# One hybrid convolution, scan and spectral block: the third image's block products split by source, the last block in two halves, and a wider carry on GpSimd

## The chip, the cores and the metric

The kernel runs on one core of one Trainium2 chip. The metric is device time in microseconds (us). The kernel before takes 21922.89 us, the median of three runs from 21910.68 to 21937.1; the profiled execution took 21922.63 us and its trace spans 21920.9 us.

## The reference, cut to what matters

Four images of 128 channels and 64 x 64 pixels pass through two layers. Layer 0 (group norm, two depthwise convolutions, a sort of patches, a scan with 16 states per channel) is not touched. In layer 1 each image is a row of 4096 tokens of 128 channels, and two things are computed, one after the other:

```
t = t + attn(ln(t))
    xs, z = split(ln(t) @ W_in);  delta = xs @ W_delta;  Bv = xs @ W_B;  Cv = xs @ W_C
    state[d, n] = exp(delta[d] * A[d, n]) * state[d, n] + delta[d] * Bv[n] * xs[d]   # token by token
    y[d] = sum over n of state[d, n] * Cv[n];   out = (y * silu(z)) @ W_out
t = t + stu(ln(t))
    U[k] = causal convolution of the tokens with filter phi[:, k], k = 0..15, and the same with
           alternating signs
    out  = sum over k of U_plus[k] @ M_plus[k] + U_minus[k] @ M_minus[k]   (+ a 3-tap term)
```

There are 256 x 256 states per token. The causal convolution of 4096 tokens is done as block products: output block `blk` (1024 tokens) takes a product with each source block from 0 to `blk`.

## The kernel before, in words

**The loop over scans.** After layer 0, `layer1` takes each image in eight chunks of 512 tokens, so 32 "parts" in all, and each part in 256 steps, one for each of 256 channels d. A step is one scan instruction on VectorE over 2 x 512 elements (L1110, `s<-da,v`): 128 partitions by two halves hold the 256 states, and 512 tokens run along the row. 8192 steps make the main loop. For every step other engines make its inputs ahead of it:

- SyncE fetches a broadcast row of `delta` for two steps (`dlb<-delta`, L1084, four buffers), issued eight steps ahead.
- GpSimd multiplies it with `u` into `v` for two steps (`spread`, L1098, one instruction over 128 x 2044 elements, three buffers), four steps ahead. ScalarE then puts the first column of each row into `v` (L1102).
- ScalarE makes the factors `da` by two exponentials (`lift`, L1107), one step ahead, in two PSUM buffers.
- The state crosses from one part to the next in `last`. `carry` (L1092, L1093) folds it into `af` and `vf` on GpSimd, 32 channels at a time, six steps ahead, so eight times in every part but the first of an image.

After each group of eight steps TensorE contracts the scanned states with `C` (L1127, `yp<-s,c`), ScalarE copies the result out (L1133, `ye`, one buffer), and a DMA stores it (L1134).

**The work beside it.** A generator, `beside`, does the projections of the next part and the output of the last one in small pieces between the steps. A piece of kind "free" is given at any step, one of kind "mm" only at the seventh step of a group of eight. Layer norms (`normalise`) go through GpSimd for the power -0.5 (L772, L773) and then on ScalarE (L777), two "free" pieces later.

**The spectral work.** When the output of a second chunk is done, `block` puts tasks on a queue. A task is (image, block, sources, partly, full): `partly` says that a sum from an earlier task is added at its end, `full` that the block is complete after it; a task that isn't full writes its sum to DRAM. A task has 64 items (2 rows r x 16 filters x 2 sides). An item is, for each source, four conv matmuls of up to 512 columns (L1058) against a strip of the filter from DRAM (L975, three buffers); then a copy of the PSUM tile on ScalarE (L1069), and one matmul with the mixing matrix `pq` (L969, five buffers) into `fin` (L1002). Images 0 to 2 take all sources of a block in one task, so nothing of block 3 can start before the image's last chunk is through. The last image (`b == NB - 1`) takes most sources as tasks of their own, so that work on blocks 2 and 3 starts with block 0. The products of the source that is the block itself are triangular: 512, 384, 256 and 128 columns.

**What sets the order.** The order is written out by hand: the engines run their instructions in the order in which this Python loop emits them. At each step the loop takes matmuls from the generator `products` until a credit is used up. The credit is `pace` x 512 columns a step, with pace 1.4 for parts 0 to 19 and 1.7 from part 20 on. After the last step, `go_on` emits what is left of the queue; this stretch, after the last scan, is called the tail below. All loads go through the one SyncE queue in program order.

Of the kernel before, what the change touches and what calls it, by code (L numbers as in the profile page):

```python
# [8 lines left out]
F32 = mybir.dt.float32  # L9
# [6 lines left out]
NB = 4  # L16
# [591 lines left out]
TS = 512  # L608
NCH = L // TS
NT = TS // 128  # L610
GD = 8
# [78 lines left out]
def layer1(ctx: ExitStack, tc, ident, half, w_in, w_delta, w_b, w_c, w_out, a_t, phi, pqd, mud, x2, x3, out):  # L690
# [66 lines left out]
    def normalise(t):  # L757

        st = sm.tile([128, NT, 6], F32, tag="st", name="st")
        mv = sm.tile([128, NT, 2], F32, tag="mv", name="mv")  # L760
        for i in range(NT):
            nc.vector.bn_stats(st[:, i, :], t[:, i, :])
        for i in range(NT):
            nc.vector.bn_aggr(mv[:, i, :], st[:, i, :])
        yield "free"
        ve = sm.tile([128, NT], F32, tag="ve", name="ve")
        nc.scalar.activation(ve, mv[:, :, 1], AF.Identity, bias=eps)
        ms = sm.tile([128, NT], F32, tag="ms", name="ms")
        nc.scalar.activation(ms, mv[:, :, 0], AF.Copy, scale=-1.0)
        yield "free"  # L770
        rs = sm.tile([128, NT], F32, tag="rs", name="rs")
        nc.gpsimd.tensor_tensor(rs, ve, half[:, :NT], ALU.pow)  # L772
        nc.gpsimd.tensor_tensor(ms, ms, rs, ALU.mult)  # L773
        yield "free"
        yield "free"
        for i in range(NT):
            nc.scalar.activation(  # L777
                t[:, i, :], t[:, i, :], AF.Identity, bias=ms[:, i : i + 1], scale=rs[:, i : i + 1]
            )
# [91 lines left out]
    def output(b, ch, yt, gate):  # L871


        cols = bass.ts(ch, TS)
        xr = small()
        nc.sync.dma_start(xr, x2[b][:, cols])
        yk = wide()
        nc.sync.dma_start(yk, gate)
        for k in range(2):
            yield "mm"  # L880
            ps = middle()
            for i in range(NT):
                nc.tensor.transpose(ps[:, bass.ts(i, 128)], yt[:, i, bass.ts(k, 128)], ident)
            yield "post"
            nc.vector.tensor_tensor(yk[:, k, :], ps, yk[:, k, :], ALU.mult)
        yield "mm"
        ps = middle()
        for k in range(2):
            nc.tensor.matmul(ps, wo[:, k, :], yk[:, k, :], start=k == 0, stop=k == 1)
        yield "post"  # L890
        nc.vector.tensor_tensor(xr, xr, ps, ALU.add)
        yield "mm"
        pair = xr.rearrange("p (a q) -> p q a", q=2)
        tp = middle()
        for r in range(2):
            for i in range(2):
                nc.tensor.transpose(tp[:, bass.ts(2 * r + i, 128)], pair[:, r, bass.ts(i, 128)], ident)
        yield "post"
        tk = small()
        nc.scalar.copy(tk, tp)  # L900
        yield "free"
        yield from normalise(tk.rearrange("p (i c) -> p i c", i=NT))
        yield "mm"
        if ch % 2 == 0:
            tokens[b, ch // 2] = sp.tile([128, 2, 4, 128], F32, tag="tok", name="tok", bufs=5)
        tok = tokens[b, ch // 2]
        ps = middle()
        nc.tensor.matmul(ps, flip, tk, start=True, stop=True)
        yield "post"
        nc.scalar.copy(tok[:, :, bass.ts(ch % 2, 2), :], ps.rearrange("p (r i c) -> p r i c", r=2, i=2))  # L910
        yield "mm"
        up = middle()
        for i in range(NT):
            nc.tensor.transpose(up[:, bass.ts(i, 128)], tk[:, bass.ts(i, 128)], ident)
        mu = sm.tile([128, 3, 128], F32, tag="mu", name="mu", bufs=1)
        nc.sync.dma_start(mu, mud[:, (0, 1, 2, 2, 3, 3, 3, 3)[ch]])
        yield "post"
        ut = sm.tile([128, 2 + TS], F32, tag="ut", name="ut", bufs=1)
        nc.scalar.copy(ut[:, 2:].rearrange("p (a q) -> p q a", q=2), up.rearrange("p (q a) -> p q a", q=2))
        if ch:  # L920
            nc.scalar.copy(ut[:, 0:2], halo)
        else:
            nc.scalar.activation(ut[:, 0:2], ident[:, 0:2], AF.Copy, scale=0.0)
        nc.scalar.copy(halo, ut[:, TS:])
        yield "mm"
        ps = middle()
        for i in range(3):
            nc.tensor.matmul(ps, mu[:, i, :], ut[:, bass.ds(2 - i, TS)], start=i == 0, stop=i == 2)
        yield "post"
        nc.vector.tensor_tensor(xr, xr, ps, ALU.add)  # L930
        nc.sync.dma_start(x3[b][:, cols], xr)
        if ch % 2:
            block(b, ch // 2)


# [8 lines left out]
    def block(b, blk):  # L944


        if b < NB - 1:
            tasks = [(b, blk, range(blk + 1), False, True)]
        else:
            tasks = (  # L950
                [(b, 0, [0], False, True), (b, 2, [0], False, False), (b, 3, [0], False, False)],
                [(b, 1, [0, 1], False, True), (b, 2, [1], True, False), (b, 3, [1], True, False)],
                [(b, 2, [2], True, True), (b, 3, [2], True, False)],
                [(b, 3, [3], True, True)],
            )[blk]
        for task in tasks:
            queue.extend(
                (task, r, k, side, src) for r in range(2) for k in range(NK) for side in range(2) for src in task[2]
            )

    def load(i):

        (b, blk, sources, _, _), r, k, side, src = queue[i]
        if src == sources[0]:
            segs = (0, 2) if blk == 0 else (min(blk + 1, 3), 1)
            pq = sp.tile([128, 2, 128], F32, tag="pq", name="pq", bufs=5)
            nc.sync.dma_start(pq[:, 0 : segs[1]], pqd[k, side][:, bass.ds(*segs)])  # L969
            mats[i] = pq  # L970
        lo = max(0, 512 * (blk - src) - 384)
        width = 896 if src < blk else 512
        strip = sp.tile([128, 896], F32, tag="strip", name="strip")
        start = (NK + k) * row + r if side else k * row + 1
        nc.sync.dma_start(strip[:, :width], bass.AP(phi.tensor, start + lo, [[1, 128], [1, width]]))  # L975
        strips[i] = strip, lo

    def products():
# [5 lines left out]

        def finish(item):
            nonlocal fin, xo, sofar
            (b, blk, _, partly, full), r, k, side, pq, u = item
            for job in [j for j in later if j[1] is u]:
                later.remove(job)
                job[2]()  # L990
            begin, end = (k, side) == (0, 0), (k, side) == (NK - 1, 1)
            cost = TS
            if begin:
                for job in [j for j in later if j[1] == "sum"]:
                    later.remove(job)
# [2 lines left out]
                if full and r == 0:  # L998
                    xo = sp.tile([128, 2 * TS], F32, tag="xo", name="xo", bufs=1)
                    nc.sync.dma_start(xo, x3[b][:, bass.ts(blk, 2 * TS)])  # L1000
            for n, (c0, w) in enumerate([(0, 256), (256, 256)] if blk == 0 else [(0, 512)]):
                nc.tensor.matmul(  # L1002
                    fin[:, bass.ds(c0, w)], pq[:, n, :], u[:, bass.ds(c0, w)],
                    start=begin and n == 0, stop=end and not partly, skip_group_check=True,
                )
# [23 lines left out]
        while True:  # L1029
# [15 lines left out]
            while issued < len(queue) and issued < i + 3:  # L1045
                load(issued)
                issued += 1
            task, r, k, side, src = queue[i]
            b, blk, sources = task[:3]
            if src == sources[0]:  # L1050
                pq = mats.pop(i)
                ps = pc.tile([128, TS], F32, tag="conv", name="conv")
            strip, lo = strips.pop(i)
            tok = tokens[b, src]
            for j in range(4):
                skip = 128 * j if src == blk else 0
                c0 = 512 * (blk - src) - 128 * j + skip
                nc.tensor.matmul(  # L1058
                    ps[:, skip:], tok[:, 1 - r if side else r, j, :], strip[:, bass.ds(c0 - lo, TS - skip)],
                    start=src == sources[0] and j == 0, stop=src == sources[-1] and j == 3,  # L1060
                )
                if j < 3:
                    yield TS - skip
            i += 1
            if src == sources[-1]:
                u = sp.tile([128, TS], F32, tag="conved", name="conved")

                def empty(u=u, ps=ps):
                    nc.scalar.copy(u, ps)  # L1069

                later.append((now[0] + 1, u, empty))
                before, waiting = waiting, ((task, r, k, side, pq, u), now[0] + 1)
# [14 lines left out]
    def carry(ch, d, ready):  # L1087

        af, vf = ready[4:]
        cols = bass.ds(d, 32)  # L1090
        if ch:
            nc.gpsimd.tensor_tensor(af[:, :, cols], af[:, :, cols], last[:, :, cols], ALU.mult)  # L1092
            nc.gpsimd.tensor_tensor(vf[:, :, cols], vf[:, :, cols], af[:, :, cols], ALU.add)  # L1093
# [21 lines left out]
    def contract(s, c, g, keep):  # L1115
# [13 lines left out]
                    )  # L1129

        def put(j):
            ye = wk.tile([128, 2, 32, GD], F32, tag="ye", name="ye", bufs=1)
            nc.scalar.copy(ye, yp[j].rearrange("p i d t -> p i t d"))  # L1133
            nc.sync.dma_start(yd[0:128, 2 * j : 2 * j + 2], ye)  # L1134

# [53 lines left out]
                    done[m] = big.tile([128, NT, 256], F32, tag="yt", name="yt", bufs=1)  # L1189
                take(done[m])  # L1190

    for k in range(-8, steps):
        now[0] = k
        j = k + 8
        if 0 <= j < steps and j % VD == 0:
            dls[j // VD] = fetch(j % 256, ready[j // 256])
        j = k + 6
        if 0 <= j < steps and j % 32 == 0:
            carry(parts[j // 256][1], j % 256, ready[j // 256])
        j = k + 4  # L1200
        if 0 <= j < steps and j % VD == 0:
# [23 lines left out]
            kind = next(side, None)  # L1225
        if at_step == GD - 1:
            fetch_y(n, d)
        pace = 1.4 if n < 5 * NCH // 2 else 1.7
        credit = min(credit + pace * TS, pace * TS)
        while credit > 0:  # L1230
            cost = next(spectral)
# [96 lines left out]
```

## Time and profile before

| stage (from the trace) | us |
|---|---|
| layer 0 and spectral weights, up to the first spread of layer 1 | 2935.7 |
| main loop, first spread to the end of the last one | 18625 |
| tail, from the last contraction (`yp`) to the end | 351 |

| engine | busy, share of the span |
|---|---|
| VectorE (DVE) | 20589.4 us, 94% |
| GpSimd (POOL) | 20181.2 us, 92% |
| TensorE (PE) | 17505.8 us, 80% |
| ScalarE (ACT) | 15831.5 us, 72% |

The shares are averages over stages that have different limits, so they do not say which engine sets the pace. In the stages of the main loop VectorE and GpSimd are both close to full, and which of the two waits for the other has to be read from the waits. In the tail neither works. In a line of the trace an instruction's idle time before it stands in brackets with what ended it; matmuls stand as two records each[...], so that a count of 8 conv records is four matmuls.

### The profile page before, as it was taken

The numbers are of one execution on the slowest core, as the hardware profiler recorded it, in microseconds if no ns is written. First come the engines' busy times: TensorE is split into PE (matmuls) and PEld (weight loads), VectorE is DVE, ScalarE is ACT, GpSimd is POOL, SyncE is SP. The second block draws the span as 40 slices with busy tenths as digits, with TensorE's granted clock in tenths as the row PEclk, the third lists the DMA queues.
The fourth block names the chain that finished last, engine by engine and source line by source line (L and its number), as shares of the span: only waits on it lengthen the run. The fifth ranks groups of instructions, "written<-read, shape, count | busy, mean of one in ns | idle before, by whom it ended". The sixth has DMA issues, their size and how long they took to land.

```text
span 21920.9 us, 291965 instructions
## 1 busy us (share of the span) xinstructions
PE 17505.8 (80%) x98516; PEld 7675.8 (35%) x98516; DVE 20589.4 (94%) x11984; ACT 15831.5 (72%) x29148; POOL 20181.2 (92%) x5932
## 2 busy tenths in 40 slices
PE   7788844565858888877768888869498899999999
PEld 4344311232323333333323333324143344334344
DVE  6788979999999999999999999999999999999993
ACT  3677757777777777777777777777777777777773
POOL 0677769999999999999999999999999999999993
PEclk8999966676979999988979999979699999999999
DMA  0455544555756776666656777757477777777775
GB/s 31 123 139 140 140 143 150 168 181 159 215 171 217 219 222 216 219 206 193 200 185 215 221 218 219 220 180 228 154 232 217 225 232 233 231 231 230 229 227 152
DMA packets 2399968, 4238.08 MB, mean 193 GB/s; under 512 B 778200, under 2 KB 1235968, under 8 KB 2395136
## 3 DMA queue, kind: packets, MB, share of 16 engines
q1 hardware_dynamic: 2398464, 4219.40, 62.8%
q8 instruction: 776, 12.71, 0.2%
q14 instruction: 728, 5.96, 0.1%
HBM read 3600.52 MB, written 617.88 MB: 192 GB/s over the span
## 4 chain that ended last, share of the span: by engine, by line
DVE 50%; POOL 17%; PE 11%; ACT 9%; issue 7%; DMA 3%; SPq 0%; DVEq 0%; POOLq 0%; ACTq 0%
DVE s L1110 43%; POOL v L1098 17%; ACT da L1107 6%; PE conv L1058 5%; DVE states L506 3%; DMA yd<-ye 2%; PE yp L1127 2%; DVE p L510 1%; PE fin L1002 1%; ACT f L498 1%; PE y L522 1%; PE mm L415 1%; ACT t L777 0%; ACT ye L1133 0%; ACT xz L362 0%
## 5 line engine op out<-in xcount | busy, mean ns | idle before, releaser
L1098 POOL TENSOR_TENSOR v<-u,dlb 128x2044 f32<-128x2044 f32 x4096 | 18342.6, 4524 | 108.9 <-DMA dlb<-delta 89.9
L1110 DVE TENSOR_TENSOR_SCAN s<-da,v 128x1024 f32<-128x1024 f32 x8192 | 18055.4, 2269 | 384.0 <-ACT da L1107 309.2
L1107 ACT ACTIVATE da<-dlb,at 128x511 f32<-128x511 f32 x16384 | 11299.4, 690 | 2064.5 <-DVE s L1110 1599.6
L1058 PE MATMUL conv<-strip,tok 128*128 128x512 f32 (+3 forms) x20480 | 8653.9, 552 | 6.7 <-DMA strip<-in_phi 6.6
L1127 PE MATMUL yp<-s,c 128*32 128x256 f32 x65536 | 5011.0, 437 | 2958.7 <-DVE s L1110 1611.9
L1058 PEld LDWEIGHTS conv<-strip,tok 128*128 128x128 f32 x20480 | 3696.9, 193 | 4126.2 <-issue 3743.4
L1127 PEld LDWEIGHTS yp<-s,c 128*32 128x32 f32 x65536 | 1990.3, 121 | 6745.9 <-issue 1835.0
L1102 ACT COPY v<-vf 128x4 f32<-128x4 f32 x4096 | 813.3, 199 | 2262.8 <-DVE s L1110 2139.2
L484 POOL TENSOR_TENSOR v<-dx,bcb 128x1024 f32<-128x1024 f32 x512 | 1207.3, 2358 | 434.5 <-DVE states L506 427.6
L1002 PE MATMUL fin<-conved,pq 128*128 128x512 f32 (+1 forms) x3200 | 1423.6, 540 | 13.2 <-ACT conved L1069 4.4
L506 DVE TENSOR_TENSOR_SCAN states<-f,v 128x1024 f32<-128x1024 f32 x512 | 1175.9, 2297 | 173.1 <-ACT f L498 124.3
L1133 ACT COPY ye<-yp 128x512 f32<-128x512 f32 x2048 | 1185.9, 579 | 136.2 <-DMA yd<-ye 123.4
L498 ACT ACTIVATE f<-dt,an 128x255 f32<-128x255 f32 x2048 | 973.5, 476 | 419.0 <-DVE states L506 368.2
L522 PE MATMUL y<-p,ident 128*128 128x512 f32 x2048 | 1008.7, 622 | 147.3 <-DVE p L510 142.2
L1069 ACT COPY conved<-conv 128x512 f32<-128x512 f32 x1344 | 778.1, 579 | 340.4 <-PE conv L1058 339.4
L510 DVE TENSOR_TENSOR p<-states,bcb 128x1024 f32<-128x1024 f32 x512 | 627.0, 1225 | 39.3 <-DVE states L506 0.9
L1002 PEld LDWEIGHTS fin<-conved,pq 128*128 128x128 f32 x3200 | 533.3, 195 | 227.1 <-issue 165.8
L522 PEld LDWEIGHTS y<-p,ident 128*128 128x128 f32 x2048 | 370.2, 196 | 680.5 <-issue 355.7
L415 PE MATMUL mm<-ow,yg 128*32 128x128 f32 x2048 | 282.1, 297 | 106.8 <-ACT om L419 105.3
L415 PEld LDWEIGHTS mm<-ow,yg 128*32 128x32 f32 x2048 | 236.2, 139 | 213.0 <-ACT om L419 128.4
L136 POOL TENSOR_TENSOR rs<-sq,half 128x1 f32<-128x1 f32 x4 | 2.2, 559 | 329.6 <-DVE sq L134 329.6
L1018 DVE TENSOR_TENSOR xo<-xo,fin 128x512 f32<-128x512 f32 x32 | 21.3, 667 | 300.8 <-PE fin L1010 300.8
(239 smaller groups left out, 6143.4 us busy)
## 6 DMA issues: line engine op xcount, KB each, us to landing
dlb<-delta SPq DMA_DIRECT2D x4096, 512.0 KB, 4.1
strip<-in_phi SPq DMA_DIRECT2D x1536, 448.0 KB, 4.8
yd<-ye SPq DMA_DIRECT2D x2048, 256.0 KB, 4.0
bcb<-bcd SPq DMA_DIRECT2D x1024, 256.0 KB, 4.2
strip<-in_phi SPq DMA_DIRECT2D x1024, 256.0 KB, 4.3
pq<-pqd SPq DMA_DIRECT2D x1088, 64.0 KB, 3.9
yt<-yd SPq DMA_DIRECT2D x4096, 4.0 KB, 3.4
pq<-pqd SPq DMA_DIRECT2D x256, 128.0 KB, 4.1
```

What stands on the lines that cost most here:

```text
L484: nc.gpsimd.tensor_tensor(v, ready[n][2][:, :, bass.ts(i, SUB)].unsqueeze(1).broadcast_to((128, 2, 2, SUB)), bc[:, 0].unsqueeze(2).broadca ...
L498: nc.scalar.activation(factors[j % 2][:, a, k, 1:], ready[n][1][:, k, SUB * i + 1 : SUB * i + SUB], AF.Exp, scale=an[:, k, 2 * g + a : 2 * ...
L506: nc.vector.tensor_tensor_scan(states.rearrange(flat), factors[j % 2].rearrange(flat), v.rearrange(flat), 0.0, ALU.mult, ALU.add)
L510: nc.vector.tensor_tensor(p, states, bc[:, 1].unsqueeze(2).broadcast_to((128, 2, 2, SUB)), ALU.mult)
L522: nc.tensor.matmul(t.rearrange("p k t -> p (k t)"), ident, p[:, a].rearrange("p k t -> p (k t)"), start=g == 0 and a == 0, stop=False, ski ...
L1002: nc.tensor.matmul(fin[:, bass.ds(c0, w)], pq[:, n, :], u[:, bass.ds(c0, w)], start=begin and n == 0, stop=end and not partly, skip_group_ ...
L1058: nc.tensor.matmul(ps[:, skip:], tok[:, 1 - r if side else r, j, :], strip[:, bass.ds(c0 - lo, TS - skip)], start=src == sources[0] and j ...
L1098: nc.gpsimd.tensor_tensor(v[:, :, :, 1:], ready[0][:, :, 1:].unsqueeze(1).broadcast_to((128, VD, 2, TS - 1)), dl[:, :, 1:].unsqueeze(2).br ...
L1107: nc.scalar.activation(da[:, h, 1:], dl[:, d % VD, 1:], AF.Exp, scale=at[:, h, d : d + 1])
L1110: nc.vector.tensor_tensor_scan(s[:, d % GD].rearrange("p h t -> p (h t)"), da.rearrange("p h t -> p (h t)"), v[:, d % VD].rearrange("p h t ...
L1127: nc.tensor.matmul(yp[i // 2][bass.ts(q, 32), i % 2], c[:, h, t], s[:, :, h, t], start=h == 0, stop=h == 1)
L1133: nc.scalar.copy(ye, yp[j].rearrange("p i d t -> p i t d"))
```

## The change

The change has six edits:

1. The third image's blocks are queued as the last image's are, source by source, so that its products can start sooner (`b < NB - 2`).
2. In the last image, block 3's own source is taken in two halves: its first two token groups (j = 0, 1) are queued when chunk 6 is done, and only the other two (j = 2, 3), which reach columns 256 to 511 alone, are left for after chunk 7. The queue's tasks now name for each source which j they take.
3. The pace is 1.7 from part 16 on (`2 * NCH`), not from part 20.
4. `carry` takes 128 channels at once, not 32, ten steps ahead.
5. `ye` has two buffers (the pool's number), and `pq` four, not five.
6. `normalise` waits five "free" pieces, not two, between GpSimd's power and ScalarE's use of it.

```diff
@@ normalise
-        yield "free"
-        yield "free"
+        for _ in range(5):
+            yield "free"
@@ output
-        if ch % 2:
+        if (b, ch) == (NB - 1, NCH - 2):
+            add([(b, 3, [(3, range(2))], True, False)])
+        elif (b, ch) == (NB - 1, NCH - 1):
+            add([(b, 3, [(3, range(2, 4))], True, True)])
+        elif ch % 2:
             block(b, ch // 2)
@@ block
-        if b < NB - 1:
+        if b < NB - 2:
             tasks = [(b, blk, range(blk + 1), False, True)]
@@ load
-            pq = sp.tile([128, 2, 128], F32, tag="pq", name="pq", bufs=5)
+            pq = sp.tile([128, 2, 128], F32, tag="pq", name="pq", bufs=4)
@@ products
+            first = 128 * sources[0][1][0] if sources[0][0] == blk else 0
...
-            for n, (c0, w) in enumerate([(0, 256), (256, 256)] if blk == 0 else [(0, 512)]):
+            for n, (c0, w) in enumerate([(0, 256), (256, 256)] if blk == 0 else [(first, TS - first)]):
...
-            for j in range(4):
+            for j in js:
...
-                    nc.scalar.copy(u, ps)
+                    nc.scalar.copy(u[:, cols], ps[:, cols])
@@ carry
-        cols = bass.ds(d, 32)
+        cols = bass.ds(d, 128)
@@ put
-            ye = wk.tile([128, 2, 32, GD], F32, tag="ye", name="ye", bufs=1)
+            ye = wk.tile([128, 2, 32, GD], F32, tag="ye", name="ye")
@@ the loop
-    for k in range(-8, steps):
+    for k in range(-10, steps):
...
-        j = k + 6
-        if 0 <= j < steps and j % 32 == 0:
+        j = k + 10
+        if 0 <= j < steps and j % 128 == 0:
             carry(parts[j // 256][1], j % 256, ready[j // 256])
...
-        pace = 1.4 if n < 5 * NCH // 2 else 1.7
+        pace = 1.4 if n < 2 * NCH else 1.7
```

More of the change, by code (lines that the diff above doesn't have):

```diff
@@ L955, in block, with add @@
             )[blk]
+        add([(b, blk, [(src, range(4)) for src in srcs], *rest) for b, blk, srcs, *rest in tasks])
+    def add(tasks):
         for task in tasks:
             queue.extend(
-                (task, r, k, side, src) for r in range(2) for k in range(NK) for side in range(2) for src in task[2]
+                (task, r, k, side, n)
+                for r in range(2) for k in range(NK) for side in range(2) for n in range(len(task[2]))
             )
     def load(i):
-        (b, blk, sources, _, _), r, k, side, src = queue[i]
-        if src == sources[0]:
+        (b, blk, sources, _, _), r, k, side, which = queue[i]
+        src = sources[which][0]
+        if which == 0:
             segs = (0, 2) if blk == 0 else (min(blk + 1, 3), 1)
-            pq = sp.tile([128, 2, 128], F32, tag="pq", name="pq", bufs=5)
+            pq = sp.tile([128, 2, 128], F32, tag="pq", name="pq", bufs=4)
             nc.sync.dma_start(pq[:, 0 : segs[1]], pqd[k, side][:, bass.ds(*segs)])
@@ L986, in finish @@
             nonlocal fin, xo, sofar
-            (b, blk, _, partly, full), r, k, side, pq, u = item
+            (b, blk, sources, partly, full), r, k, side, pq, u = item
+            first = 128 * sources[0][1][0] if sources[0][0] == blk else 0
             for job in [j for j in later if j[1] is u]:
@@ L991, in finish @@
             begin, end = (k, side) == (0, 0), (k, side) == (NK - 1, 1)
-            cost = TS
+            cost = TS - first
             if begin:
@@ L1047, in products @@
                 issued += 1
-            task, r, k, side, src = queue[i]
+            task, r, k, side, which = queue[i]
             b, blk, sources = task[:3]
-            if src == sources[0]:
+            src, js = sources[which]
+            final = which == len(sources) - 1
+            if which == 0:
                 pq = mats.pop(i)
@@ L1059, in products, with empty @@
                     ps[:, skip:], tok[:, 1 - r if side else r, j, :], strip[:, bass.ds(c0 - lo, TS - skip)],
-                    start=src == sources[0] and j == 0, stop=src == sources[-1] and j == 3,
+                    start=which == 0 and j == js[0], stop=final and j == js[-1],
                 )
-                if j < 3:
+                if j < js[-1]:
                     yield TS - skip
             i += 1
-            if src == sources[-1]:
+            if final:
                 u = sp.tile([128, TS], F32, tag="conved", name="conved")
-                def empty(u=u, ps=ps):
-                    nc.scalar.copy(u, ps)
+                cols = bass.ds(first := 128 * js[0] if src == blk else 0, TS - first)
+                def empty(u=u, ps=ps, cols=cols):
+                    nc.scalar.copy(u[:, cols], ps[:, cols])
                 later.append((now[0] + 1, u, empty))
```

## The prediction

> **What bounds the kernel now.** I first cut the span into stages by windows: parts 16 to 19, 24 to 27 and 28 to 31 of the main loop, then the tail. The columns are length, busy time of TensorE, its weight loads, VectorE, ScalarE, GpSimd, then the granted TensorE clock, the DMA share and GB/s.
>
> ```profile
> 12249.00:14569.00 2320.00, 1948.35 (x11678) 833.25 (x11670) 2280.40 (x1133) 1742.84 (x3228) 2315.31 (x578) 0.95 0.69 215
> 16902.00:19236.00 2334.00, 2150.10 (x12244) 935.41 (x12244) 2277.73 (x1133) 1778.21 (x3303) 2317.01 (x578) 0.97 0.74 228
> 19236.00:21566.00 2330.00, 2208.08 (x12308) 931.67 (x12312) 2281.84 (x1119) 1820.27 (x3372) 2315.74 (x588) 0.99 0.74 228
> 21566.00:21922.00 356.00, 346.55 (x1060) 180.21 (x1052) 5.29 (x14) 62.31 (x111) 1.22 (x2) 0.99 0.42 115
> ```
>
> In the loop GpSimd is busy 99.2 to 99.8% of the time, VectorE about 98%. In the tail only TensorE is (97%). Who follows whom in the loop is told by the groups of GpSimd and by the waits, both from the first scan to the last spread (the waits start with the first spread, whose wait of 42.8 us is a start-up):
>
> ```profile
> L1098 POOL TENSOR_TENSOR v<-u,dlb 128x2044 f32<-128x2044 f32 x4096 | 18342.6, 4524 | 108.9 <-DMA dlb<-delta 89.9 <-DVE s L1110 15.9 <-POOL v L1098 2.6
> L1092 POOL TENSOR_TENSOR af<-af,last 128x64 f32<-128x64 f32 x224 | 74.2, 331 | 0.0
> L1093 POOL TENSOR_TENSOR vf<-vf,af 128x64 f32<-128x64 f32 x224 | 71.5, 319 | 17.5
> L772 POOL TENSOR_TENSOR rs<-ve,half 128x4 f32<-128x4 f32 x62 | 63.4, 1023 | 0.0
> L773 POOL TENSOR_TENSOR ms<-ms,rs 128x4 f32<-128x4 f32 x62 | 12.5, 202 | 4.9
> ```
>
> ```profile
> DVE s L1110 <- ACT da L1107: 309.2, 160, 5.8
> DVE s L1110 <- POOL v L1098: 64.9, 99, 7.9
> ...
> ACT ye L1133 <- DMA yd<-ye: 121.2, 91, 5.8
> ACT t L777 <- POOL ms L773: 117.4, 56, 3.2
> ACT v L1102 <- POOL vf L1093: 114.6, 96, 1.4
> ```
>
> GpSimd waits for VectorE only 15.9 us in 18,625. So GpSimd is the metronome: 4096 spreads at 18342.6/4096 = 4.48 us are 98.5% of the loop, and whatever else stands in its queue is paid in full. VectorE needs 18055.4/4096 = 4.41 us for the same pair of steps, and has other work and waits on ScalarE of 309.2 us: it is second by a small margin, and that is the first doubt below.
>
> In the tail I read the timeline, just before the end. Two records are one matmul.
>
> ```profile
> 21880.46 1.02 PE L1002 MATMUL fin<-conved,pq 128*128 128x512 f32 x2
> 21880.65 0.33 SPq L975 DMA_DIRECT2D strip<-in_phi  x1
> 21881.32 2.32 PE L1058 MATMUL conv<-strip,tok 128*128 128x512 f32 x8
> 21881.51 0.32 SPq L969 DMA_DIRECT2D pq<-pqd  x1
> 21883.47 1.02 PE L1002 MATMUL fin<-conved,pq 128*128 128x512 f32 x2
> ```
>
> An item of the last task (conv 512+384+256+128 columns, fin 512: 1792) repeats every 21883.47 - 21880.46 = 3.01 us, or 0.86 us for 512 columns, which I call a unit. TensorE has no gap. The strip is asked for when a buffer comes free and lands 3.3 us later (median in the tail; 4.3 us in the loop), two items ahead.
>
> **What the Trainium skill says.** (1) "GPSIMD Engine Reference", section "3.1 Elementwise": a two-input tensor_tensor over 2048 fp32 elements takes 4497 ns, at a cost per element. The trace agrees: 4524 ns for 2044. So the spread is at its own price. (2) "SBUF — State Buffer", section "Who interferes with whom": VectorE contends with GpSimd's reads only with two SBUF inputs or in a two-port mode. The scan reads `da` from PSUM, so a closer packed VectorE shouldn't lengthen the spread; in the loop its duration stays between 4479 and 4639 ns, which fits. (3) "DMA: Bandwidth & Descriptors", section "Anatomy of one DMA": about 2 us of a transfer are fixed, whatever its size. The tail's 3.3 us for 256 KB agrees in kind, so halving an item's matmuls doesn't shorten its load. (4) "TensorE: Matmul & The Clock Gate", Part 1: an idle window of some 3.4 us halves the clock. The tail agrees: after a wait of 3.27 us at 21580 four conv records take 3.28 us, against 1.98 us for four before it.
>
> **The change part by part.**
>
> *Wider carry.* It removes 8 carries from each of 28 parts, 224 in all, and adds 2 a part, 56. One carry now costs GpSimd (74.2 + 71.5 + 17.5)/224 = 0.73 us. The wide one's instructions have 256 elements, not 64; no row shows this size. Bounds: 0.33 us each if size cost nothing, 4 x 0.33 = 1.32 us if all scaled. Between, I add 192 elements at 4524/2044 = 2.2 ns: 0.33 + 0.42 = 0.75 us, so 1.58 us a carry with the gap. Saved: 163 - 56 x 1.58 = 163 - 88 = 75 us (bounds 163 - 41 = 122 and 163 - 152 = 11). It lies on the bounding engine. The new place, ten steps ahead, waits for nothing: `last` for those channels was written over 100 steps earlier, and the next part's `af` is finished, in the order of the built program, at step 194 of a part, 52 steps before the carry that reads it.
>
> *Buffers of ye, pieces of normalise, carry further ahead.* They take away ScalarE's waits of 121.2, 117.4 and 114.6 us. ScalarE isn't the bound, so this is no gain itself; but its delays are what VectorE waits for (309.2 us), and they are what VectorE needs to lose if it is to follow a faster GpSimd. Direct gain: part of the 66 us that GpSimd waits in the loop beyond the start-up. These waits are on `dlb`, whose loads stand in SyncE's queue behind others, mostly bursts when an output ends; the bursts stay. I take 5 us.
>
> *Third image by source, pace 1.7.* Both add no scan work. In the order of the built program TensorE has 1.40 units a step in parts 16 to 18 before and 1.70 after, as it already has in parts 27 to 31 before. There, a step costs 1.7 x 0.86 = 1.46 us plus 8 contractions (about 0.5 us) and projections, inside a step of 2.28 us; the fourth window shows that 95% busy TensorE at clock 0.99 stands beside a GpSimd at 99.4%. No VectorE wait for TensorE's release of `s` shows. 320 more items' fin matmuls (five more tasks) bring 320 copies of 0.58 us on ScalarE (78% busy in the dense stage), and 320 loads of `pq`: hidden by the spread. Parts 20 to 31 last 583.0 us on average and parts 1 to 19 without the image starts 582.4, so I charge the dense parts 1 us each, 6 us in all. What it gains is the backlog: before, the third image's products still fill part 26; after, the queue runs dry in part 24, so the last image starts with an empty queue.
>
> *Tail.* In the built order, after the last contraction stand 398 units of TensorE work before (340 us, of the 351) and 324 after. The 324 are 242 units of backlog, output work and first half, and 82 of the second half with its two sums. The first: 242 x 0.86 = 207 us, plus 7 us of waits in the last output as before. The second: each item is conv 256 + 128 and fin 256 columns, 640 in all, 1.07 us of TensorE. But each needs a strip of 256 KB and a `pq`. With three strip buffers and now four of `pq`, loads for item i+2 start only when fin of item i-2 is done: SyncE issues pq (0.4 us), then the strip, which lands 3.3 us after. From that fin to the next conv are three items less its own conv and fin: 3T - 1.07 = 3.8, T = 1.62 us, so the wait for strips takes the place of TensorE. 64 x 1.62 = 104 us. Bounds: 64 x 1.07 = 69 us if the loads keep up, 64 x (4.8 + 1.07)/3 = 125 us at the loop's landing time of 4.3. End (addition and store) 4 us. Sum: 207 + 7 + 104 + 4 = 322 us (287 to 343), against 351: 29 us less (8 to 64).
>
> Sum: 75 + 5 - 6 + 29 = 103 us. 21923 - 103 = 21820 us.
>
> **Rivals.**
>
> A, VectorE takes over as the bound. Its own need for a part is about 564 us of scans, 6 of other work, and 10 of waits for `da`: 580, no less than GpSimd's 580.5 now. For it: 16 waits of GpSimd for VectorE occur already. Against it: parts without a carry (8 and 16) last 577 us, so VectorE can go there, and the waits on ScalarE are being cut. If VectorE allows 1 us a part of the 2.7, the loop gives 28 us, and the tail 29 less the 6 of the dense parts: 21923 - 51 = 21872 us.
>
> B, more than that: the tail at TensorE's own pace (64 us less) and half of GpSimd's 66 us of waits gone with ScalarE's: 75 + 33 + 64 - 6 = 166, 21757 us.
>
> C, slower: the dense third image (more loads on one SyncE queue, `strip` waits of 570 us in the loop already, each holding back the `dlb` behind it) makes eight parts 15 us longer and the last image's 6 dense ones 5, 150 us in all, against 103: 21970 us. For it: part 26, where a new image's tasks start at pace 1.7, lasts 587.5 us, 5 more than others. Against it: the parts around it are at 582 to 583.
>
> **How the numbers follow.** Forecast 0.60, A 0.20, B 0.13, C 0.07. The predicted time is the forecast's, 21820. The range goes from 21765, near B, to 21885, past A, and leaves out C and the far end of B. A change under 0.2% (44 us) needs A with a poor tail, or a mild C: 0.08. Faster 0.87, slower 0.05.
>
> **What would show it.** Right: 112 carry instructions of 128x256 at about 0.75 us; GpSimd still busy 99% of the loop and waiting little for VectorE; carry parts of about 579 us; ScalarE's three waits gone; the queue dry in part 24; in the tail's second half, items every 1.6 us with conv waiting for the strip. Wrong: GpSimd waiting for `s` by more than 50 us (A); conv without gaps at the end (B); `dlb` waits over 150 us or a scan waiting for TensorE in parts 16 to 23 (C); wide carries at 1.3 us would halve the gain.

## The result, and the profile after

The changed kernel takes 21811.96 us (median of four runs, 21809.69 to 21814.77), against 21924.06 us in the runs before it was set beside: a ratio of 0.9949, interval 0.9932 to 0.9966. It is 112 us faster; 103 us were forecast, 21820 us.

The sum was nearly right, but two of its terms were not. Cut at the first spread, the end of the last spread and the end:

| stage, us | before | after | difference | forecast |
|---|---|---|---|---|
| up to the first spread | 2935.7 | 2940.9 | +5 | 0 |
| main loop | 18625.4 | 18518.8 | -107 | -74 |
| tail after the last contraction | 350.6 | 344.2 | -6 | -29 |

(Between the last spread and the last contraction lie 9 us in both. The start is untouched code: in the kernels below, it lies between 2929 and 2942 us, so some 6 us of any single trace are chance.)

First the windows of the kernel after: parts 16 to 19, 24 to 27 and 28 to 31, then the tail. The columns are as before: length, TensorE, weight loads, VectorE, ScalarE, GpSimd, TensorE clock, DMA share, GB/s.

```profile
12196.30:14513.00 2316.70, 2213.30 (x12508) 963.39 (x12507) 2285.95 (x1135) 1782.79 (x3312) 2312.43 (x544) 1.00 0.76 235
16826.00:19140.00 2314.00, 1812.64 (x11274) 801.96 (x11273) 2283.95 (x1133) 1805.80 (x3361) 2309.84 (x543) 0.87 0.66 204
19140.00:21460.00 2320.00, 2205.47 (x12302) 929.43 (x12301) 2284.70 (x1120) 1822.99 (x3376) 2311.66 (x541) 0.99 0.75 229
21460.00:21813.00 353.00, 302.77 (x982) 161.73 (x980) 9.56 (x16) 76.25 (x158) 1.22 (x2) 0.98 0.57 148
```

Parts 16 to 19 are now as dense on TensorE (96%) as parts 28 to 31, without a longer loop; in parts 24 to 27 TensorE falls to 78%, since the queue runs dry in part 24. GpSimd is still the full engine. New is the last line: in the tail TensorE is busy 86%, where it was 97%. Then GpSimd's groups in the loop, and the waits of VectorE and of GpSimd (us in total, times, longest):

```profile
L1112 POOL TENSOR_TENSOR v<-u,dlb 128x2044 f32<-128x2044 f32 x4096 | 18335.5, 4535 | 70.5 <-DMA dlb<-delta 63.3 <-DVE s L1124 7.1
L1106 POOL TENSOR_TENSOR af<-af,last 128x256 f32<-128x256 f32 x56 | 42.3, 755 | 0.0
L1107 POOL TENSOR_TENSOR vf<-vf,af 128x256 f32<-128x256 f32 x56 | 40.7, 726 | 4.4
```

```profile
DVE s L1124 <- ACT da L1121: 117.2, 77, 10.1
DVE s L1124 <- POOL v L1112: 81.4, 78, 8.0
```

```profile
POOL v L1112 <- DMA dlb<-delta: 63.3, 9, 42.7
...
POOL v L1112 <- DVE s L1124: 7.1, 5, 4.6
```

The wide carries cost 0.755 and 0.726 us, as estimated (0.75). The surprise is in the waits: VectorE's for `da` fell from 309 to 117 us, and GpSimd's, less the start-up of 43 us in both, from 66 to 28 us: a fall of 38 where I had allowed 5. The tail's second half, from its timeline:

```profile
21713.21 0.89 PE L1071 MATMUL conv<-strip,tok 128*128 128x256 f32 x4 [0.38 <-DMA strip<-in_phi]
21713.23 0.42 SPq L985 DMA_DIRECT2D strip<-in_phi  x1
21713.94 0.60 PE L1013 MATMUL fin<-conved,pq 128*128 128x256 f32 x2
21714.57 0.32 SPq L979 DMA_DIRECT2D pq<-pqd  x1
21714.69 0.89 PE L1071 MATMUL conv<-strip,tok 128*128 128x256 f32 x4 [0.15 <-DMA strip<-in_phi]
...
21716.95 0.89 PE L1071 MATMUL conv<-strip,tok 128*128 128x256 f32 x4 [0.94 <-DMA strip<-in_phi]
```

The strip issued at 21713.23 is for the third conv of these lines, which starts 3.72 us later, after a wait on it. So the loads set the pace of the 64 short items; they take 124 us, 1.93 us each in the mean (1.77 in the median), where TensorE alone would need 1.09.

### The profile page after: what moved, and what is told of

Read it like the earlier page. It is cut to its first block, busy times and chain, and to the rows that moved or that the text cites. A ratio compares the mean times of both kernels' runs of the same rounds, so it can differ in the third digit from the quotient of the medians.

```text
span 21813.1 us, 294297 instructions
## 1 busy us (share of the span) xinstructions
PE 17725.7 (81%) x99308; PEld 7769.6 (36%) x99308; DVE 20650.6 (95%) x11984; ACT 16013.9 (73%) x29544; POOL 20126.2 (92%) x5596
## 4 chain that ended last, share of the span: by engine, by line
DVE 48%; POOL 21%; PE 12%; ACT 8%; issue 6%; DMA 3%; SPq 0%; DVEq 0%; POOLq 0%; ACTq 0%
DVE s L1124 41%; POOL v L1112 20%; PE conv L1071 5%; ACT da L1121 5%; DVE states L506 3%; PE yp L1141 2%; DVE p L510 1%; PE fin L1013 1%; ACT f L498 1%; DMA dlb<-delta 1%; PE y L522 1%; PE mm L415 1%; DMA strip<-in_phi 1%; DMA yd<-ye 0%; ACT xz L362 0%
## 5 line engine op out<-in xcount | busy, mean ns | idle before, releaser
L1013 PE MATMUL fin<-conved,pq 128*128 128x512 f32 (+1 forms) x3968 | 1792.2, 544 | 17.7 <-ACT sum L1034 6.2
L1083 ACT COPY conved<-conv 128x512 f32<-128x512 f32 (+1 forms) x1728 | 987.1, 571 | 332.8 <-PE conv L1071 331.5
L1013 PEld LDWEIGHTS fin<-conved,pq 128*128 128x128 f32 x3968 | 666.4, 192 | 395.9 <-issue 286.1
```

The source lines that it names most:

```text
L1013: nc.tensor.matmul(fin[:, bass.ds(c0, w)], pq[:, n, :], u[:, bass.ds(c0, w)], start=begin and n == 0, stop=end and not partly, skip_group_ ...
L1083: nc.scalar.copy(u[:, cols], ps[:, cols])
```

## The experiments

Each was timed beside the kernel before, and its ratio is to that kernel. Where a number of a stage is given, it is from the kernel's own trace, cut as above.

**Which edit shortened the loop?** Four kernels start from the one before.

The wider carry alone:

```diff
-        cols = bass.ds(d, 32)
+        cols = bass.ds(d, 128)
...
-        j = k + 6
-        if 0 <= j < steps and j % 32 == 0:
+        j = k + 10
+        if 0 <= j < steps and j % 128 == 0:
```

> The kernel before with the wider carry alone (128 channels, ten steps ahead). Theory M, GpSimd sets the pace of the loop: 224 carries of 0.73 us become 56 of about 1.56 us, so the loop (first spread to end of the last) is 76 us shorter, plus a little where ScalarE no longer waits for the carry; the tail is unchanged at 351 us; about 21845 us. Theory A, VectorE would take over if ScalarE's waits were not cut too: the loop gains 40 us or less and GpSimd waits for VectorE 50 us or more; about 21885 us.

Measured: ratio 0.9979 (0.9971 to 0.9987), loop 18585.7 us, 40 us shorter; tail 350.7. The waits of GpSimd and VectorE in its loop:

```profile
POOL v L1098 <- DMA dlb<-delta: 98.4, 22, 42.6
POOL v L1098 <- DVE s L1110: 25.6, 34, 5.0
POOL v L1098 <- POOL v L1098: 6.6, 14, 0.8
POOL v L1098 <- issue: 4.0, 3, 1.7
```

```profile
DVE s L1110 <- ACT da L1107: 286.0, 176, 5.2
```

This is nearer to theory A in its size (40 us, the most that A allowed) though the waits for VectorE stay under A's 50. The carries themselves cost 76 us less, as in the changed kernel, but GpSimd's waits beyond the start-up rose by 26 us, to 92. And 17 us of the 76 had never been in the loop: consecutive GpSimd instructions overlap a little (a spread lasts 4.52 us in the kernel before, and the next starts 4.47 us after it), so that the busy times and waits of GpSimd's groups add to 27 us more than the loop in the kernel before, and only 11 here. 76 - 26 - 17 = 33 us, and 6 us less of busy time in the spreads, make the 40.

The buffers of `ye` and the pieces of `normalise`, together and each alone:

```diff
-            ye = wk.tile([128, 2, 32, GD], F32, tag="ye", name="ye", bufs=1)
+            ye = wk.tile([128, 2, 32, GD], F32, tag="ye", name="ye")
...
-            pq = sp.tile([128, 2, 128], F32, tag="pq", name="pq", bufs=5)
+            pq = sp.tile([128, 2, 128], F32, tag="pq", name="pq", bufs=4)
```

```diff
-        yield "free"
-        yield "free"
+        for _ in range(5):
+            yield "free"
```

> The kernel before with two buffers of ye, four of pq, and five free pieces in normalise, alone. Theory M as predicted: ScalarE is not the bound, so its waits of 121 and 117 us go away and the time falls by about 5 us. Revised theory M2, from the trace of the changed kernel: ScalarE's stalls reach GpSimd through late delta rows and full v buffers, so GpSimd's 66 us of waits in the loop fall to about 45 and the loop is 20 us shorter. Built order has 411 units of TensorE work after the last contraction, 13 more than before, so the tail is 11 us longer: about 21914 us by M2, 21929 by M.

> The kernel before with two buffers of ye and four of pq alone (normalise as before). Theory Y: of the 42 us by which both edits shorten the loop, most comes from ye, because ScalarE's wait for the store of ye (up to 5.8 us) stops the exponentials, and so the release of delta rows to GpSimd: loop 30 us shorter, GpSimd's waits from 66 to about 35 us, tail unchanged, about 21890 us. Rival N, most comes from normalise: loop 10 us shorter, about 21912 us.

> The kernel before with five free pieces in normalise, in place of two, alone. Theory N: ScalarE's in-order wait for GpSimd's power (117 us in 56 waits of about 2 us) holds up the exponentials behind it, so that VectorE falls behind; with ye alone the loop gained 7 us of the 42 that both give, so this alone gives 30 to 35 us: VectorE's waits for da fall from 309 to about 130 us, GpSimd's waits from 66 to about 35, and with 13 more units of tail (11 us) the time is about 21901 us. Rival: the two edits only work together, and this alone gives less than 15 us, 21915 us or more.

| alone | ratio (interval) | loop, us | change of loop | VectorE's wait for da | tail |
|---|---|---|---|---|---|
| both | 0.9985 (0.9978 to 0.9992) | 18583.5 | -42 | 97 | 362.9 |
| ye | 0.9996 (0.9987 to 1.0005) | 18618.0 | -7 | 282 | 351.8 |
| normalise | 0.9985 (0.9978 to 0.9992) | 18581.0 | -44 | 166 | 363.3 |

M's 5 us are refuted, M2's 20 are too few, and wrong too was my first thought that `ye` mattered most: `normalise` alone does it all, and `ye` adds nothing to it that can be measured. Its waits, with those of the kernel before repeated in the prediction:

```profile
POOL v L1098 <- DMA dlb<-delta: 65.0, 11, 42.7
POOL v L1098 <- DVE s L1110: 1.5, 3, 0.9
```

```profile
DVE s L1110 <- ACT da L1107: 165.5, 115, 4.8
```

How ScalarE's wait reaches GpSimd is seen in the kernel before: ScalarE stands in its order for the power, and the exponentials stand behind.

```profile
14669.35 1.41 ACT L1107 ACTIVATE da<-dlb,at 128x511 f32<-128x511 f32 x2
14670.69 0.20 ACT L1138 COPY last<-s 128x16 f32<-128x16 f32 x1
14673.86 1.65 ACT L777 ACTIVATE t<-t,ms,rs 128x128 f32<-128x128 f32 x4 [2.97 <-POOL ms L773]
14675.42 1.39 ACT L1107 ACTIVATE da<-dlb,at 128x511 f32<-128x511 f32 x2
```

The next pair of exponentials starts 6.1 us after the last pair, where a step of the loop has 2.3. The rows of `delta` are released by these exponentials, and SyncE holds the next fetch until then (in the kernel before it waits for them 8422 us in all). The runs show the total effect on GpSimd's waits (66 us to 24); that each wait for `dlb` comes by this path I have not traced. The 12 us more of tail are 13 more units that the later projections leave at the end.

The third image by source and pace 1.7 from part 16, alone:

```diff
-        if b < NB - 1:
+        if b < NB - 2:
...
-        pace = 1.4 if n < 5 * NCH // 2 else 1.7
+        pace = 1.4 if n < 2 * NCH else 1.7
```

> The kernel before with the third image by source and pace 1.7 from part 16, alone. The built order has 276 units after the last contraction, against 398. Theory M: the tail falls by 122 x 0.86 = 104 us to about 247, since the last task, 64 items of 3.02 us, is not bound by loads; the loop changes by less than 10 us, with some 14 us of GpSimd's waits in parts 20, 22 and 24 gone since the queue no longer runs dry there: about 21810 us. Rival C, the dense third image slows the loop: parts 16 to 23 are 5 us or more longer, 21860 us.

Measured: ratio 0.9960 (0.9945 to 0.9975), loop 18632.1 us, 7 us longer, tail 254.1, 97 us shorter. Theory M holds; C, the slower loop, does not show: parts 16 to 23 are within 4 us of before, but for part 16 (8 us longer). The time, 21837 us, is 27 us above M's all the same: the tail is 7 us longer than M has it, and GpSimd's waits beyond the start-up did not fall (71 us, 66 before). So this edit alone takes over three times as much from the tail as was forecast for the whole change. Why then is the changed kernel's tail only 6 us shorter?

**The half sources.** The changed kernel without them, and the kernel before with them alone. In the first, `output` ends as before:

```diff
-        if (b, ch) == (NB - 1, NCH - 2):
-            add([(b, 3, [(3, range(2))], True, False)])
-        elif (b, ch) == (NB - 1, NCH - 1):
-            add([(b, 3, [(3, range(2, 4))], True, True)])
-        elif ch % 2:
+        if ch % 2:
             block(b, ch // 2)
```

> The changed kernel without the half sources: block 3's own source is one task again, everything else as changed. The built order has 290 units after the last contraction, against 324, and none of them is of the short items. Theory T, the half sources cost time here, because the queue is not empty at the end of the loop and the short items are bound by the landing of their strips: the tail is 290 x 0.86 + 11 = 260 us, not 344, and the time falls by 84 us to about 21728. Rival, the halves save what they take out of the tail: the time rises to about 21840 us or more.

> The kernel before with the half sources alone. The built order has 432 units after the last contraction, against 398, 82 of them the short items. Theory T, no unit of the first half is done before the loop ends, because the queue is never empty there: the tail is 350 units at 0.86 us, 11 us of waits and end, and 64 short items at about 1.5 us (five pq buffers, so a strip waits only for its own buffer), about 410 us in all, 60 us more than before; the loop is unchanged: about 21985 us. Rival: the first half runs under the loop and the tail shrinks by 80 us or more.

Measured without them: ratio 0.9909 (0.9892 to 0.9925), 21722.96 us, 89 us faster than the changed kernel; loop 18519.5, tail 259.9. With them alone: ratio 1.0032 (1.0020 to 1.0044), slower; loop 18617.2, tail 421.3. Theory T is right in both to 11 us. The tail without them is TensorE's again (96% busy):

```profile
21458.00:21718.00 260.00, 250.91 (x784) 136.93 (x780) 5.29 (x14) 48.94 (x88) 1.22 (x2) 0.99 0.41 111
```

The first half can be done early only if TensorE reaches it before the loop ends. It doesn't: 242 of the 324 units left are in front of the second half, the whole first half among them: the trace of the changed kernel's tail has 76 items whose `fin` has 512 columns, the 64 of the first half and 12 older ones, and then the 64 short ones. So the edit adds 34 units (a second set of fin matmuls and sums) and turns the last items into short ones that wait for loads.

**What bounds the short items?** From here on the kernels start from the changed one. First, strips of 256 columns where no more are read, and `pq` in eight tiles of 64 KB:

```diff
-        width = 896 if src < blk else 512
+        width = 896 if src < blk else TS - 128 * sources[which][1][0]
...
-            pq = sp.tile([128, 2, 128], F32, tag="pq", name="pq", bufs=4)
+                pq = sp.tile([128, 128], F32, tag="pq", name="pq", bufs=8)
```

> The changed kernel, with strips of 256 columns in place of 512 for the second half, and pq in tiles of 64 KB, eight of them, so that no load waits for the mixing matmul. Theory T, the short items are bound by landing time over three strip buffers: (0.4 + 3.1 + 0.6)/3 = 1.3 to 1.4 us an item, not 1.93, so the tail is about 35 us shorter than 344 and the time about 21777 us; the loop is unchanged. Rival, the items are bound by TensorE and ScalarE's copies: no change, 21812 us.

Measured: ratio 0.9939 (0.9925 to 0.9954), 21784.71 us; tail 319.4, 25 us shorter. A short item now takes 1.47 us (median), not 1.77. Half the bytes land in 3.3 us, not 3.7 (medians): most of the landing time does not go with the bytes here, and three buffers divide it. But this run has two edits, and the strips are not all of the gain. The kernel with the half sources alone has the long strips, but still five buffers of `pq`. What SyncE waits for in the short items, in the changed kernel and then in that one:

```profile
SPq L979 <- PE fin L1013: 63.0, 59, 5.0
```

```profile
SPq L985 <- PE conv L1071: 43.5, 61, 2.1
```

With four, SyncE stands for a `pq` buffer (L979), which only `fin` releases, and the strip's load stands behind it; with five, it stands for the strip's own buffer (L985), and a short item takes 1.60 us (median). So the `pq` buffer that edit 5 gave up costs about 0.17 us an item, some 11 us of the changed kernel's tail by this estimate; that kernel with five was not run.

Then two short strips in one buffer, so that six items can be under way (with the paces below, which leave a short tail):

```diff
-            while issued < len(queue) and issued < i + 3:
+            while issued < len(queue) and issued < i + (5 if queue[i][0][2][0][1][0] else 3):
...
+        for n in range(2 if width < 512 else 1):
+            start = (NK + k) * row + r if side or n else k * row + 1
+            part = strip[:, bass.ds(n * width, width)]
+            nc.sync.dma_start(part, bass.AP(phi.tensor, start + lo, [[1, 128], [1, width]]))
+            strips[i + n] = part, lo
```

> The kernel of pace 1.8 with two short strips in one buffer, so that six short items can be under way in the three buffers, and pace 2.0 in the last part, which has no projections. The built order has 184 units after the last contraction. Theory T: with the loads far enough ahead a short item takes TensorE's own 1.1 us, so the tail is (184 - 82) x 0.86 + 11 + 64 x 1.1 + 6 = about 175 us, against 244, and the loop 8 us longer: about 21665 us. Rival: the short items are bound by SyncE's issue of two loads each (0.75 us) or by something else and stay at 1.5 us: about 21690 us.

Measured: ratio 0.9893 (0.9879 to 0.9908), 21687.36 us, the fastest of all with its variant below; tail 185.5, loop 18550.3. In most of the second half its timeline has a short item every 1.09 us (the median too), which is TensorE's own time, and no wait:

```profile
21606.89 0.60 PE L1019 MATMUL fin<-conved,pq 128*128 128x256 f32 x2
21607.33 0.81 PE L1077 MATMUL conv<-strip,tok 128*128 128x256 f32 x4
21607.98 0.60 PE L1019 MATMUL fin<-conved,pq 128*128 128x256 f32 x2
```

Theory T is shown: with the same bytes, the same number of loads and the same matmuls as in the kernel of pace 1.8 below, where an item takes 1.47 us, the item falls to TensorE's own time, and TensorE's waits for strips fall from 15.0 us to 4.1. A load even takes longer to land, 4.3 us (median). So what held the short items was how many loads were in flight. The total missed by 22 us, since the last part at pace 2.0 lasted 597 us, not 576.

**How dense may TensorE be beside the scans?** The pace in the last image's parts, here 1.8 (then 1.9, and 1.85 with 2.0 in the last part), on the kernel with short strips; the reset keeps the end going when the queue has run dry:

```diff
-        pace = 1.4 if n < 2 * NCH else 1.7
+        pace = 1.4 if n < 2 * NCH else 1.7 if n < 26 else 1.8
...
+    idle = 0
     while idle < 8:
```

> The kernel of e6 with pace 1.8 in the last image's dense parts (26 to 31). The built order has 235 units after the last contraction, against 324. If the loop bears it (theory M: TensorE has 5% idle there), the tail is 89 x 0.86 = 76 us shorter than in e6, about 232 us, and the time about 21700 us. Rival: TensorE becomes the bound in parts 26 to 31, which lengthen by 10 us or more each, and the gain is lost.

> The same with pace 1.9: 141 units after the last contraction. By theory M the tail is 157 us shorter than in e6, about 150 us, and the loop a little longer: about 21630 us. Rival: a step's TensorE work, 1.9 x 0.86 + 0.5 + projections, is 2.26 us and more, just a step of the loop, so the scans wait for TensorE, parts 26 to 31 lengthen by 15 to 30 us each, and the time is 21720 us or more.

> The same with pace 1.85 in parts 26 to 30: 149 units after the last contraction, 30 us of tail less. Between pace 1.8, which lengthened the loop by 6 us, and 1.9, by 73 us: if the loss sets in where TensorE's step reaches that of the loop, 1.85 costs about 15 us and the time is about 21650 us; if it grows from 1.8 on in a straight line, it costs 34 us, and the time is about 21669 us.

| pace, parts 26 to 31 | median, us | ratio (interval) | loop | tail |
|---|---|---|---|---|
| 1.7 (short strips) | 21784.71 | 0.9939 (0.9925 to 0.9954) | 18525.5 | 319.4 |
| 1.8 | 21725.72 | 0.9913 (0.9896 to 0.9929) | 18531.6 | 243.9 |
| 1.9 | 21709.66 | 0.9905 (0.9891 to 0.9920) | 18598.8 | 163.3 |
| 1.8, then 2.0; paired strips | 21687.36 | 0.9893 (0.9879 to 0.9908) | 18550.3 | 185.5 |
| 1.85, then 2.0; paired strips | 21686.65 | 0.9893 (0.9878 to 0.9908) | 18579.9 | 157.1 |

Pace 1.8 costs the loop 6 us for 76 of tail; 1.9 costs 73 for 156. The forecasts were lower: 21700 us for 1.8, and for 1.9 either 21630 or, if the scans waited for TensorE, 21720 or more; 21710 is close to the second. Pace 1.85 was to give 21650 or 21669 us and brought nothing: against 1.8 it lengthened the loop by 30 us for 28 less of tail. Windows of about part 27 at pace 1.7 (the changed kernel), 1.8 and 1.9:

```profile
18562.00:19140.00 578.00, 552.49 (x2992) 219.27 (x2991) 569.94 (x282) 461.67 (x863) 577.69 (x136) 1.00 0.74 232
```

```profile
18560.00:19140.00 580.00, 571.65 (x3040) 228.83 (x3036) 569.28 (x283) 463.92 (x867) 577.38 (x136) 1.00 0.74 235
```

```profile
18520.00:19100.00 580.00, 576.22 (x3000) 231.87 (x2999) 551.17 (x275) 448.68 (x846) 561.48 (x133) 1.00 0.74 232
```

TensorE goes from 96 to 99% busy, and at 1.9 GpSimd drops from 100 to 97%: it has begun to wait for the scans (66.5 us in all), and 275 VectorE instructions are done in the window where 282 and 283 were. Here TensorE has become the bound of the loop, and it reaches the scans through ScalarE. The wait of ScalarE for the products, from 18000 us to the last spread, at pace 1.9:

```profile
ACT conved L1085 <- PE conv L1073: 271.1, 307, 3.2
```

It is 36.4 us in the changed kernel and 84.7 at 1.8. VectorE waits for ScalarE's exponentials 115.1 us in this stretch (35.6 in the changed kernel), and for TensorE itself 5.3. So it looks like the stall of `normalise` again: ScalarE stands in its order for another engine, and the exponentials stand behind. That each of these waits is passed on so is not traced.

At these paces the half sources may pay after all. Without them the last task alone leaves 64 items of 1792 columns, 224 units, for the time after the loop; the two kernels with paired strips have 184 and 149 units left there. They were not run without the half sources, so this stays open.

## Why the prediction was right, and where its steps failed

- *The bound.* Right: GpSimd sets the pace of the loop, and what leaves its queue shortens it. Spreads started 4.47 us apart before and after (mean of those back to back), whatever VectorE did.
- *Wider carry.* The size of the instruction was right (0.74 us against 0.75), and so was what it takes off GpSimd's busy time and gaps (76 us, forecast 75). As a gain of the loop it was over-sized: alone it gave 40 us. The step took a group's time for the loop's; overlap of instructions took 17 us, and 26 us came back as GpSimd's own waits while ScalarE's stalls lasted.
- *ScalarE's waits.* The step that failed: "Direct gain ... I take 5 us". `normalise` alone gave 44 us of loop. I put the waits for `dlb` down to SyncE's bursts alone; the run shows that most of them go away when ScalarE no longer stands still for GpSimd's power. The sentence before it, that these waits are what VectorE must lose to follow a faster GpSimd, held: carry alone 40, both ScalarE edits alone 42, and the changed kernel 107 (with the third image, which alone cost 7): some 30 us more than their sum. No run has the two together without the third image.
- *Third image.* Right in its parts: TensorE hid it, and C fell. In the tail, 97 us were its own, of 104 by units.
- *Tail.* Forecast 29 us less, bounds 8 to 64, measured 6. The 242 units took 213 us with their waits, forecast 214. The second half took 124 us and not 104: the term T was 1.62 us and is 1.93. (Its own terms, 0.4 and 3.3, add to 3.7 and not to the 3.8 of the sum, which makes 1.59 us and 102 us; the miss is then 22 us.) The strip landed 3.7 us after its issue, not 3.3 as with longer items; an item's own time to the end of fin is 1.33 us, not 1.07; and the waits at the start and for the partial sums are in the mean: by these figures three buffers give (0.4 + 3.7 + 1.33)/3 = 1.81 us, and the median is 1.77. Worse than the size: I compared the two tails as wholes and so did not see that the half sources cost 84 us of the 97 that the third image brought.
- *Rival A* does not hold for the changed kernel (GpSimd waits 7 us for VectorE), but a part of it showed where the carry was changed alone (26 us, 16 before). *B* had the right size for ScalarE's part (33 us; the waits fell by 38) and the wrong one for the tail.

So the total came out within 8 us because two errors, 33 us too little in the loop and 23 too much in the tail, nearly cancelled. That closeness is luck; that GpSimd sets the pace, and that the short items wait for their strips, is not.

## What to carry to other kernels

In the changed kernel, splitting the last task to start it early could not pay, because more work than its first half was still queued when the loop ended; count the units still in front of it at the loop's end, and cost each edit's tail alone. When items get shorter, divide the landing time of a load by the number of buffers and compare it with the item. An engine in second place that waits in its order for another can cost the bounding one time: here moving the use later gave as much of the loop as cutting the bounding engine's own work, and the two together more.

## What the runs showed of the hardware that was not expected

A 128-partition load of 128 KB landed in 3.3 us (median) where one of 256 KB took 3.7, in the same stage; with up to six strips in flight and not three, one of 128 KB took 4.3. TensorE kept a clock of 0.98 to 0.99 in the second half of the changed kernel's tail although it was busy only 86 of 124 us: gaps that were mostly under 1 us did not lower it. One gap there did: after a wait of 3.36 us at 21692 the next four short conv records took 1.62 us and not 0.82, and the clock was 0.79 from 21690 to 21698.
